# Attention outputs of two sequences times their output weights: seven quarter products in place of eight

## The chip, the core and the metric

The kernel runs on one core of a Trainium2 chip. The metric is device time in microseconds (us) of one execution; it is compared by the median of several runs. Names of engines: PE is the matrix engine (TensorE), DVE is VectorE, ACT is ScalarE, POOL is GpSimd, SP is SyncE, which here only starts transfers. "SPq" or "POOLq" in a row is that engine's sequencer starting a DMA.

## The reference

Eight sequences of 128 tokens with 512 features go through three layers. A per-sequence adapter (one 512x512 matrix chosen by an id) is followed by a base product with eight gated low-rank experts; then comes attention with 32 query heads and 8 key/value heads over a paged cache of 512 positions and the 128 new ones, with its output product; then a bottleneck feed-forward layer with 64 gated experts. Everything is float32. The part that the change touches is the last line of attention:

```python
scores = jnp.einsum('bqhd,bkhd->bhqk', q, k_all) * SCALE
scores = jnp.where(valid[:, None, None, :], scores, -1e+30)
probs = jax.nn.softmax(scores, axis=-1)
o = jnp.einsum('bhqk,bkhd->bqhd', probs, v_all)
o = o.reshape(bsz, seqlen, HQ * D)
return jnp.einsum('bse,de->bsd', o, Wo)
```

With `bsz` 8, `seqlen` 128, `HQ` 32, `D` 128, the last line multiplies, for each sequence, a 128x4096 matrix by a 4096x512 matrix.

## The kernel before

**Units.** Attention is cut into 64 units `u`. A unit is one sequence and one key/value head with its 4 query heads (`REP`). The heads are taken in 4 passes (`NQ`); a pass handles 2 key/value heads (`GH`) of all 8 sequences, so a pass has 16 units, and a step `st = u // 2` is one sequence in one pass. Four units with `u % 4` = 0, 1, 2, 3 are therefore two sequences with two heads each; this group has number `k = u // 4`, 16 of them. In what follows c stands for `u % 4`.

**The order.** No scheduler decides: each engine gets its instructions in the order in which the Python code records them, and works through them in that order. `iteration(u)` records, with a software pipeline over units: the page fetches of the next step's keys (`gather`, L194, on SP; 10 pages in even units and 6 in odd ones, three of them ahead of `exchange_in`), the transfers that bring the previous unit's transposed probabilities back (`exchange_in`, L893 and L896, on SP), the value rows (`gather_v`, L204, on POOL), the rotation tables for an odd unit (`make_tables`, L233, on POOL), in even units the load of the output sums of two steps ahead (`load_y`, L143, on SP), and the eviction of the attention output of unit u-3 (`evict_o`, L927, on ACT).

Then four head slots h = 0 to 3 follow. In each: the score matmuls (`scores`, L834 for the 512 cached keys, L837 for the 128 new ones, into one of two PSUM buffers), masking with the row minimum on DVE (`mask_exp`, L847) and the exponential on ACT (L858), the division by the sum of the head before (`normalize`, L863 on DVE, L864 on POOL), a transpose of 32x32 blocks of the head two before (`blocks`, L869, DVE), four heads' worth of output product of unit u-3 (`output`, L938, one 128x512 matmul a slot), and up to one of the seven products that make queries, keys and values for later units (`project`, L259, 128x384, two matmuls a product; its results are added on DVE in L262). These projections are already computed as seven products of quarters for two sequences at a time; the sums of their inputs' quarters come from `sums_x` (L168 to L171, POOL, once per pair of sequences) and of their weights' quarters from `sums_q` (L163, DVE).

At the end of a unit: the last division and the last two block transposes, `norms(u+3)` (L308 on ACT, L312 and L314 on POOL), `exchange_out(u)` (L883: the transposed probabilities go to DRAM, two transfers from SP, two from ACT), `rotate(u+3)` (L326 to L344 on DVE; the step L340 waits for POOL's L314), one more projection in odd units, and `values(u-2)` (L916, ten 128x512 matmul instructions).

**The output product.** The 8 head products of a step add up in one PSUM bank (`y`). After the second head `add_output` evicts it on DVE: L955 copies in the first pass, L959 adds the sum of earlier passes that `load_y` brought from DRAM, and L962 writes the new sum to DRAM. The sum that `load_y` fetches in unit u is used in unit u+2:

```python
if u % GH == 0 and B <= st - 1 < NQ * B:
    load_y(st - 1)
```

The output weights of a head (`wo_t[g]`, 4x512 columns) sit in one of three buffers and are loaded by `load_o` (L177, POOL queue). In the program a 128x512 float32 matmul is one instruction; the trace shows two matmul records and two weight loads for each, so 256 matmuls of L938 stand there as x512.

Of the kernel before, what the change touches and what calls it, by code (L numbers as in the profile page):

```python
# [57 lines left out]
def adaln_ffn_kernel(  # L58
# [42 lines left out]


# [31 lines left out]
    xo = keep.tile([P, B // 2, 7, 2, S], F32, name="xo")  # L134
    yp = ctx.enter_context(tc.tile_pool(name="yp", bufs=3))
# [5 lines left out]
    def load_y(st):  # L141
        t = yp.tile([P, DM], F32, tag="ya", name=f"ya_{st}")
        nc.sync.dma_start(out=t, in_=y_d[st % B])  # L143
        ya_t[st] = t

    wq_t, wo_t = {}, {}
# [18 lines left out]
    def sums_x(pr):  # L165

        a = xo[:, pr].rearrange("p x c s -> p x (c s)")
        nc.gpsimd.tensor_tensor(a[:, 5], a[:, 0], a[:, 2], ALU.subtract)  # L168
        nc.gpsimd.tensor_tensor(a[:, 2], a[:, 2], a[:, 3], ALU.add)
        nc.gpsimd.tensor_tensor(a[:, 4], a[:, 2], a[:, 0], ALU.subtract)  # L170
        nc.gpsimd.tensor_tensor(a[:, 6], a[:, 1], a[:, 4], ALU.subtract)  # L171

    def load_o(g, first=0, end=REP):

        if first == 0:
            wo_t[g] = wp.tile([P, REP, DM], F32, tag="wo", name=f"wo_{g}", bufs=GH + 1)
        nc.gpsimd.dma_start(  # L177
            out=wo_t[g][:, first:end], in_=wo[g, first:end].rearrange("h p n -> p h n")
        )
# [47 lines left out]
    def make_tables(st):  # L227

        b = st % B
        t = pj.tile([P, 2, 4, D // 2], F32, tag="tab", name=f"tab_{st}", bufs=2)  # L230
        nwv = nw.rearrange("p i (t d) -> p (i t) d", t=2)
        for i, f in enumerate((cos, sin)):
            nc.gpsimd.tensor_tensor(  # L233
                t[:, i], nwv, f[:, b, :].unsqueeze(1).to_broadcast([P, 4, D // 2]), ALU.mult
            )
        tab_t[st] = t
# [12 lines left out]

    def project(k, j, products):  # L250
# [3 lines left out]
        for i in products:  # L254
# [3 lines left out]
            for c in range(2):  # L258
                nc.tensor.matmul(  # L259
                    out=ps, lhsT=xo[:, pr, x, c, :], rhs=w[:, c, :], start=(c == 0), stop=(c == 1)  # L260
# [92 lines left out]
    def transpose_qk(u, home=None):  # L353
# [7 lines left out]
        if home is None:  # L361
            home = pj.tile([P, NH * S], F32, tag="qkT", name=f"qkT_{u}", bufs=2)
# [33 lines left out]
    with ExitStack() as l0:  # L396
# [30 lines left out]
        bias = yp.tile([P, DM], F32, tag="ya", name="bias")  # L427
# [7 lines left out]
        for b in (5, 6, 7):  # L435
            wt_7 = wp.tile([P, NC, DM], F32, tag="wo", name=f"wt_{b}", bufs=GH + 1)
            wt_home[b] = wt_7
# [48 lines left out]
        ang = yp.tile([P, B, D // 2], F32, tag="ya", name="ang")  # L486
        kk = yp.tile([P, B, D // 2], F32, tag="ya", name="kk")
# [126 lines left out]
        for t in range(B):  # L614
# [34 lines left out]
            if t in (5, 6):  # L649
                make_tables(t - 5)  # L650
# [13 lines left out]
        for g in range(GH):  # L664
            load_o(g)
# [3 lines left out]
        rotate(1)  # L669
        l0_experts(B - 1)  # L670
        project_whole(1, 0, 0, 0)
        transpose_qk(1)
# [4 lines left out]
        transpose_qk(2, wt_7.rearrange("p c n -> p (c n)")[:, : NH * S])  # L677
# [110 lines left out]
    with ExitStack() as l1:  # L788
# [8 lines left out]
        p_t, pb_t, pT_t, den_t, o_t, oT_t, y_t = {}, {}, {}, {}, {}, {}, {}  # L797
# [15 lines left out]
        def blocks_qk(u, w):  # L813

            if w == 1:
                gap = xo[:, 0, 4:].rearrange("p x c s -> p (x c s)")[:, : NH * S]
# [82 lines left out]
        def heads_qk(u):  # L899

            qkT = pj.tile([P, NH * S], F32, tag="qkT", name=f"qkT_{u}", bufs=2)
# [22 lines left out]

        def evict_o(u):
            oT = wk1.tile([P, REP, S], F32, tag="oT", name=f"oT_{u}")
            nc.scalar.copy(  # L927
                oT.rearrange("p h (i a) -> p h i a", a=32),
                o_t.pop(u).rearrange("p (i h a) -> p h i a", i=QD, h=REP),
            )  # L930
            oT_t[u] = oT

        def output(u, h):
            st, g = units[u]
            j = g % GH
            if h == 0 and j == 0:
                y_t[st] = bank("y", f"y_{st}")
            nc.tensor.matmul(  # L938
                out=y_t[st],
                lhsT=oT_t[u][:, h, :],  # L940
                rhs=wo_t[g][:, h, :],
# [4 lines left out]
        def add_output(u):  # L946
            st, g = units[u]
            del oT_t[u]
            if g % GH < GH - 1:
                return  # L950
            y = y_t.pop(st)
            last = st >= (NQ - 1) * B
            if g < GH:
                ya_t[st] = yp.tile([P, DM], F32, tag="ya", name=f"ya_{st}")
                nc.vector.tensor_copy(ya_t[st], y)  # L955
            else:

                t = y_home[st % B] if last and st % B < 4 else ya_t[st]
                nc.vector.tensor_tensor(t, y, ya_t[st], ALU.add)  # L959
                ya_t[st] = t  # L960
            if not last:
                nc.sync.dma_start(out=y_d[st % B], in_=ya_t.pop(st))  # L962
# [4 lines left out]
        y_home, yT_t, room_t = {}, {}, {}  # L967
# [44 lines left out]
        spare = xo.rearrange("p r x c s -> p (r x c s)")  # L1012
        written_t = {}

        def z_blocks(b):
            if 0 <= b < TURNED:
                turn_blocks(zg_t[b], spare[:, b * DM : (b + 1) * DM])

        def z_exchange(b):

            if 0 <= b < TURNED:
                written_t[b] = turn_out(b, spare[:, b * DM : (b + 1) * DM])
# [3 lines left out]
        def iteration(u):  # L1026
# [30 lines left out]
            if u % GH == 0 and B <= st - 1 < NQ * B:  # L1057
                load_y(st - 1)
# [10 lines left out]
            for h in range(REP):  # L1069
                if on(u):  # L1070
                    scores(u, h)
                    mask_exp(u, h)
                    if h > 0:
                        normalize(u, h - 1)

                    if h == 1:
                        if u == 2:
# [19 lines left out]
                if on(u - 3):  # L1097
                    output(u - 3, h)
# [5 lines left out]
            if on(u - 3):  # L1104
                add_output(u - 3)
# [5 lines left out]
            if u < NU - 8:  # L1111
                if r in (8, 9, 10, 11):
                    load_q(group + r // 10, r % 2, r % 2 + 2)
                if r in (12, 13):
                    load_o(group, r % 2 * 2, r % 2 * 2 + 2)
# [193 lines left out]
```

## Time and profile before

| | |
|---|---|
| three runs | 1242.72, 1242.82, 1244.57 us; median 1242.82 us |
| profiled execution | 1242.47 us, span in the trace 1240.6 us |
| granted PE clock | 0.999 of full |
| PE busy | 1223.1 us (99% of the span) |
| DVE busy | 905.9 us (73%) |
| POOL busy | 588.7 us (47%) |
| ACT busy | 506.6 us (41%) |
| HBM | 243 GB/s over the span |

The profiled execution is 1.9 us longer than its span, which counts from the first to the last instruction of the program. Busy shares are means over the whole kernel; start (to 115 us), attention (115 to 1200 us) and the end (to 1240.6 us) have different limits. Rows of matmuls overlap their successors by some tenths of a us, so the cost of one is read from start to start. In a group's row the columns are line, engine, operation, output<-input, shapes, count, then busy us and mean ns, then the idle time before it with what ended it.

### The profile page before, as it was taken

Reading aid. Unit: us, or ns where it says so; the run is one execution under the profiler, and the core shown is the slowest. Engines: PE = TensorE matmul, PEld = TensorE weight load, DVE = VectorE, ACT = ScalarE, POOL = GpSimd, SP = SyncE. Lnnn points to the kernel's source line nnn. Section 1 sums busy time; section 2 is a strip of 40 time slices with the busy share of each in tenths; the row PEclk is TensorE's granted clock in tenths of the full one; section 3 lists DMA queues with packets and bytes.
Section 4 is the critical chain, followed back from the end, with each engine's and each line's share of the span. In section 5 each row is a group of like instructions: output and inputs, shape, how many; then the busy total and the mean of one; then the engine's idle time right before and its main releaser. Section 6 shows DMA issues by size and latency. Waiting matters only on the chain.

```text
span 1240.6 us, 15999 instructions
## 1 busy us (share of the span) xinstructions
PE 1223.1 (99%) x3823; PEld 648.6 (52%) x3823; DVE 905.9 (73%) x2051; ACT 506.6 (41%) x1457; POOL 588.7 (47%) x687
## 2 busy tenths in 40 slices
PE   8999899999999999999999999999999999999998
PEld 7765455554555555555555545555555555555544
DVE  2545788888877777788877777799777777787622
ACT  1344544444444444444444444444444444443211
POOL 2443565675544545555545544555545544553100
PEclk9999999999999999999999999999999999999999
DMA  8833687788878877888878877888878776888642
GB/s 303 287 96 94 218 237 247 226 282 281 272 238 256 273 246 239 276 283 278 269 260 257 259 247 248 290 280 288 261 242 280 249 237 220 258 271 268 206 126 95
DMA packets 209825, 302.14 MB, mean 244 GB/s; under 512 B 85123, under 2 KB 120708, under 8 KB 208836
## 3 DMA queue, kind: packets, MB, share of 16 engines
q1 hardware_dynamic: 178132, 208.72, 53.7%
q10 hardware_dynamic: 18720, 52.32, 12.0%
q0 software_dynamic: 12880, 40.08, 9.7%
q8 instruction: 31, 0.51, 0.2%
q14 instruction: 62, 0.51, 0.1%
HBM read 185.12 MB, written 115.93 MB: 243 GB/s over the span
## 4 chain that ended last, share of the span: by engine, by line
PE 92%; DVE 2%; DMA 1%; ACT 1%; SPq 1%; POOL 1%; issue 1%; ACTq 0%; DVEq 0%; POOLq 0%
PE o L916 20%; PE p L259 20%; PE y L938 18%; PE s L834 17%; PE s L837 4%; PE bp L546 2%; PE op L1200 2%; PE p L292 2%; PE cp L524 2%; PE fz L730 2%; DMA bww<-in_base_w 1%; DMA pT<-px 1%; PE cp L541 1%; SPq L883 1%; PE bp L587 0%
## 5 line engine op out<-in xcount | busy, mean ns | idle before, releaser
L864 POOL TENSOR_SCALAR p<-p,den 128x640 f32<-128x640 f32 x256 | 210.9, 824 | 424.3 <-DVE den L863 423.8
L858 ACT ACTIVATE p<-p,low 128x640 f32<-128x640 f32 x256 | 212.0, 828 | 433.0 <-DVE den L863 294.3
L847 DVE CUSTOM_DVE_ANT_0 p<-s,mask,rs 128x640 f32<-128x640 f32 x256 | 223.6, 879 | 109.8 <-PE s L837 106.9
L259 PE MATMUL p<-wqkv,xo 128*128 128x384 f32 x784 | 280.3, 486 | 0.0
L938 PE MATMUL y<-wo,oT 128*128 128x512 f32 x512 | 262.4, 597 | 6.3 <-ACT oT L927 6.3
L834 PE MATMUL s<-kt,qkT 128*128 128x512 f32 x504 | 258.7, 595 | 2.0 <-ACT qkT L903 1.0
L916 PE MATMUL o<-pT,vt 128*128 128x512 f32 x512 | 230.2, 592 | 0.0
L869 DVE STREAM_TRANSPOSE pb<-p 128x640 f32<-128x640 f32 x256 | 210.9, 824 | 17.7 <-POOL p L864 17.7
L259 PEld LDWEIGHTS p<-wqkv,xo 128*128 128x128 f32 x784 | 149.1, 190 | 140.1 <-issue 73.5
L837 PEld LDWEIGHTS s<-qkT 128*128 128x128 f32 x504 | 96.1, 191 | 121.1 <-issue 121.1
L916 PEld LDWEIGHTS o<-pT,vt 128*128 128x128 f32 x512 | 97.3, 190 | 110.3 <-issue 95.2
L204 POOL DMA_INDIRECT vt<-in_vc,vrow x128 | 136.0, 1063 | 39.1 <-issue 28.1
L834 PEld LDWEIGHTS s<-kt,qkT 128*128 128x128 f32 x504 | 95.1, 190 | 96.9 <-issue 53.9
L308 ACT ACTIVATE sq<-c 128x128 f32<-128x128 f32 x320 | 98.8, 309 | 8.1
L314 POOL TENSOR_TENSOR rs<-ss,mhalf 128x5 f32<-128x5 f32 x64 | 99.1, 1548 | 5.3
L837 PE MATMUL s<-qkT 128*128 128x128 f32 x504 | 97.1, 274 | 0.0
L927 ACT COPY oT<-o 128x512 f32<-128x512 f32 x64 | 37.5, 586 | 143.9 <-PE o L916 136.4
L938 PEld LDWEIGHTS y<-wo,oT 128*128 128x128 f32 x512 | 78.6, 192 | 13.2 <-ACT oT L927 8.8
L262 DVE TENSOR_TENSOR c<-c,p 128x384 f32<-128x384 f32 x84 | 45.3, 539 | 30.4 <-PE p L259 30.4
L916 PE MATMUL o<-pT,vn 128*128 128x512 f32 x128 | 65.4, 592 | 0.0
L308 ACT ACTIVATION_READ_ACCUMULATOR sq<-c 128x1 f32 x320 | 59.7, 187 | 0.0
L340 DVE SCALAR_TENSOR_TENSOR ca<-c,rs,tab 128x128 f32<-128x128 f32 x64 | 24.8, 388 | 42.2 <-POOL rs L314 42.2
(183 smaller groups left out, 1199.8 us busy)
## 6 DMA issues: line engine op xcount, KB each, us to landing
pT<-px SPq DMA_DIRECT2D x64, 1280.0 KB, 6.6
px<-pb ACTq DMA_DIRECT2D x120, 400.0 KB, 6.6
px<-pb SPq DMA_DIRECT2D x120, 400.0 KB, 5.4
qkb<-px SPq DMA_DIRECT2D x61, 320.0 KB, 3.5
kt<-in_kc SPq DMA_DIRECT2D x512, 32.0 KB, 4.4
wqkv<-in_wqkv POOLq DMA_DIRECT2D x32, 384.0 KB, 5.0
yd<-ya SPq DMA_DIRECT2D x24, 256.0 KB, 3.0
wo<-in_wo POOLq DMA_DIRECT2D x12, 512.0 KB, 4.5
```

The source lines that it names most:

```text
L204: nc.gpsimd.indirect_dma_start(out=kv_t[step][1][:, c, :], out_offset=None, in_=vc, in_offset=bass.IndirectOffsetOnAxis(ap=vrow[:, hf, at ...
L259: nc.tensor.matmul(out=ps, lhsT=xo[:, pr, x, c, :], rhs=w[:, c, :], start=(c == 0), stop=(c == 1))
L308: nc.scalar.activation(sq, cs[:, at : at + D], AF.Square, accum_out=ss[:, h : h + 1])
L314: nc.gpsimd.tensor_tensor(rs, ss, mhalf, ALU.pow)
L834: nc.tensor.matmul(out=s[:, :L], lhsT=qkT[:, h, :], rhs=kt[:, :, g % GH, :], start=True, stop=True)
L837: nc.tensor.matmul(out=s[:, L:NK], lhsT=qkT[:, h, :], rhs=qkT[:, REP, :], start=True, stop=True)
L847: nc.vector.tensor_tensor_reduce(out=p, in0=s_t.pop((u, h))[:, :NK], in1=mask_t[st], scale=rs_t[u][:, h : h + 1], scalar=BIG, op0=ALU.add, ...
L858: nc.scalar.activation(p, p, AF.Exp, bias=low, scale=-1.0, accum_out=den)
L864: nc.gpsimd.tensor_scalar(p_t[u, h], p_t[u, h], den, 1.0, ALU.mult, ALU.mult)
L869: nc.vector.transpose(pb_t[u][:, :, h * w : (h + 1) * w].rearrange("p i (j a) -> p j i a", a=32), p_t.pop((u, h)).rearrange("p (j i a) -> ...
L916: nc.tensor.matmul(out=o, lhsT=vt[:, c, j * D : (j + 1) * D] if c < LC else vn_t.pop(u), rhs=pT[:, c], start=(c == 0), stop=(c == LC),)
L938: nc.tensor.matmul(out=y_t[st], lhsT=oT_t[u][:, h, :], rhs=wo_t[g][:, h, :], start=(h == 0 and j == 0), stop=(h == REP - 1 and j == GH - 1),)
```

## The change

For 13 of the 16 groups k (all but 0, 14 and 15) the output product of two sequences and two heads is treated as a 2x2 block product, (sequences) x (heads) times (heads) x (halves of the 512 output columns), and is computed with seven products of blocks in place of eight. One product is four 128x256 matmuls (`product_y`), two in each of two head slots; 14 half products lie in 16 head slots. Products alternate between the two halves of one PSUM bank, `y_ps`, which is now one tile for all of attention. Two products are evicted by ACT copies, five by DVE additions, and POOL does two more additions on the results (`combine_y`).

The sums of blocks that the seven products need are made as follows. On the left, `sums_y` makes four sums of 128x512 a group on POOL, in a new tile `ot` with five places, one of which each `evict_o` fills. On the right, the weights of a pass are one tile `wo_t` of seven blocks of 4x256 columns, not buffered twice; `sums_o` makes four sums a pass on DVE, and `load_o` fetches four blocks a pass.

The sums of earlier passes are now added on POOL (`add_y`, 128x512) for groups 4 to 13. The sum of the first sequence of group k is loaded at the start of unit 4k+7, added at the end of unit 4k+8 and stored in 4k+9. The sum of the second is loaded at the start of unit 4k+10, behind that unit's page fetches as before, added in head slot 2 of the same unit, and stored at its end; for group 13 this is unit 61 with c = 1.

To make room, the projection's input sums move from `xo` (7 places per pair of sequences, made once) to `xs` (4 places in all, remade on POOL for each pair and pass in slots 1 and 2 of units with c = 3), the tables and the transposed queries have one buffer in place of two, and other short-lived tiles move.

```diff
+    wo_t = wp.tile([P, 7, REP, DM // 2], F32, name="wo")
...
+    def sums_x(pr, *names):
+
+        a, t = (v.rearrange("p x c s -> p x (c s)") for v in (xo[:, pr], xs))
+        for n in names:
+            to, x, y, op = {
+                3: (t[:, 2], a[:, 0], a[:, 2], ALU.subtract),
+                2: (t[:, 1], a[:, 3], t[:, 2], ALU.subtract),
+                1: (t[:, 0], t[:, 1], a[:, 0], ALU.add),
+                4: (t[:, 3], a[:, 1], t[:, 1], ALU.subtract),
+            }[n]
+            nc.gpsimd.tensor_tensor(to, x, y, op)
...
+    def sums_o(t):
+
+        to, x, y = {3: (5, 3, 1), 2: (4, 5, 0), 4: (6, 2, 4), 1: (1, 1, 0)}[t]
+        nc.vector.tensor_tensor(
+            wo_t[:, to], wo_t[:, x], wo_t[:, y], ALU.add if t == 2 else ALU.subtract
         )
...
-        t = pj.tile([P, 2, 4, D // 2], F32, tag="tab", name=f"tab_{st}", bufs=2)
+        t = pj.tile([P, 2, 4, D // 2], F32, tag="tab", name=f"tab_{st}")
...
+        def sums_y(k, n):
+
+            a = ot.rearrange("p x h s -> p x (h s)")
+            a11, a12 = a[:, k % 2], a[:, 1 - k % 2]
+            to, x, y, op = {
+                3: (a[:, 4], a11, a[:, 2], ALU.subtract),
+                1: (a[:, 2], a[:, 2], a[:, 3], ALU.add),
+                2: (a11, a[:, 2], a11, ALU.subtract),
+                4: (a[:, 4], a12, a11, ALU.subtract),
+            }[n]
+            nc.gpsimd.tensor_tensor(to, x, y, op)
...
+        def product_y(k, i, part):
...
+            ps = y_ps[:, (7 * k + order) % 2 * n :][:, :n]
+            for h in range(2 * part, 2 * part + 2):
+                nc.tensor.matmul(
+                    out=ps, lhsT=ot[:, x, h, :], rhs=wo_t[:, y, h, :], start=(h == 0), stop=(h == 3)
+                )
...
+        def add_y(k, i):
+
+            st = 2 * k + i
+            t = y_home[st % B] if st >= (NQ - 1) * B else ya_t[st]
+            nc.gpsimd.tensor_tensor(t, ya_t[st], n_t.pop((k, i)), ALU.add)
+            ya_t[st] = t
...
+            places = [(1, 4, 3), (1, 5, 1), (2, 6, 0), (2, 6, 1), (7, 6, 2), (7, 6, 3), (6, 7, 1)]
+            places += [(6, 7, 2), (5, 7, 3), (5, 8, 0), (3, 8, 1), (3, 8, 2)]
+            places += [(4, 8, 3)] * 2 if k + 1 in WHOLE_Y else [(4, 9, 2), (4, 9, 3)]
...
+        def pool_y(u, h):
+
+            seven = lambda k: 0 < k < NU // 4 - 2
+            k, c = divmod(u, 4)
+            if c == 1 and h == 1 and seven(k - 1):
+                sums_y(k - 1, 3)
+            if c == 2 and seven(k - 1):
+                if h in (1, 3, 4):
+                    sums_y(k - 1, {1: 1, 3: 2, 4: 4}[h])
+            if c == 3 and h == 3 and seven(k - 1):
+                combine_y(k - 1, 6)
+            if c == 0 and h == 1 and seven(k - 2):
+                combine_y(k - 2, 5)
+            if c == 0 and h == 4 and k - 2 >= NQ and seven(k - 2):
+                add_y(k - 2, 0)
+            last = k - 2 == NU // 4 - 3
+            if c == (1 if last else 2) and h == 2 and k - 2 >= NQ and seven(k - 2):
+                add_y(k - 2, 1)
+
+        def moves_y(u, start):
+
+            k, c = divmod(u, 4)
+            seven = lambda k: 0 < k < NU // 4 - 2
+            if start:
+                if c == 3 and k - 1 >= NQ and seven(k - 1):
+                    load_y(2 * (k - 1))
+                last = k - 2 == NU // 4 - 3
+                if c == (1 if last else 2) and k - 2 >= NQ and seven(k - 2):
+                    load_y(2 * (k - 2) + 1)
...
-            if u % GH == 0 and B <= st - 1 < NQ * B:
-                load_y(st - 1)
+            moves_y(u, True)
...
+                    pool_y(u, h)
+                    if u % 4 == 3 and 1 < (u + 5) // 4 < NU // 4 and h in (1, 2):
+                        sums_x((u + 5) // 4 % (B // 2), *((3, 2), (1, 4))[h - 1])
...
-                if on(u - 3):
-                    output(u - 3, h)
+                for f_out, args in OUT.get((u, h), ()):
+                    f_out(*args)
```

## The prediction

> **What bounds the kernel now.** I read the page first (busy shares, then the chain that ended last), then groups by shape for durations, then timelines of single engines over one unit.
>
> ```profile
> PE 1223.1 (99%) x3823; PEld 648.6 (52%) x3823; DVE 905.9 (73%) x2051; ACT 506.6 (41%) x1457; POOL 588.7 (47%) x687
> ...
> PE o L916 20%; PE p L259 20%; PE y L938 18%; PE s L834 17%; PE s L837 4%; PE bp L546 2%; PE op L1200 2%; PE p L292 2%; PE cp L524 2%; PE fz L730 2%; DMA bww<-in_base_w 1%; DMA pT<-px 1%; PE cp L541 1%; SPq L883 1%; PE bp L587 0%
> ...
> L938 PE MATMUL y<-wo,oT 128*128 128x512 f32 x512 | 262.4, 597 | 6.3 <-ACT oT L927 6.3
> ```
>
> PE is the bound, and 18% of the chain is the work that the change cuts. But a cut counts only while PE is never kept waiting, so the covers matter. PE's timeline in units 30 and 31 (unit 30 begins with its first score matmul at 605.28):
>
> ```profile
> 621.28 1.02 PE L834 MATMUL s<-kt,qkT 128*128 128x512 f32 x2
> 622.14 0.38 PE L837 MATMUL s<-qkT 128*128 128x128 f32 x2
> 622.36 1.02 PE L938 MATMUL y<-wo,oT 128*128 128x512 f32 x2
> 623.22 1.02 PE L834 MATMUL s<-kt,qkT 128*128 128x512 f32 x2
> ...
> 626.45 1.02 PE L834 MATMUL s<-kt,qkT 128*128 128x512 f32 x2
> ```
>
> From start to start two 512-column matmuls take 0.86 us, two of 128 take 0.22. SP's queue in unit 30:
>
> ```profile
> 605.52 4.13 SPq L194 DMA_DIRECT2D kt<-in_kc  x3
> 611.31 0.53 SPq L893 DMA_DIRECT2D qkb<-px  x1
> 611.89 0.63 SPq L896 DMA_DIRECT2D pT<-px  x1
> 613.03 5.40 SPq L194 DMA_DIRECT2D kt<-in_kc  x7
> 618.50 0.40 SPq L143 DMA_DIRECT2D ya<-yd  x1
> ```
>
> The load of the old output sum, recorded at the unit's start, is issued 13.2 us into a unit of 16.0, because ten page fetches and the return of the probabilities stand ahead of it. Before, that costs nothing: its user comes two units later. POOL and DVE in the same unit:
>
> ```profile
> 612.87 0.81 POOL L864 TENSOR_SCALAR p<-p,den 128x640 f32<-128x640 f32 x1 [2.42 <-DVE den L863]
> 616.12 0.81 POOL L864 TENSOR_SCALAR p<-p,den 128x640 f32<-128x640 f32 x1 [2.44 <-DVE den L863]
> 618.51 0.80 POOL L864 TENSOR_SCALAR p<-p,den 128x640 f32<-128x640 f32 x1 [1.58 <-DVE den L863]
> ```
>
> ```profile
> 618.33 0.82 DVE L869 STREAM_TRANSPOSE pb<-p 128x640 f32<-128x640 f32 x1
> 619.34 0.84 DVE L869 STREAM_TRANSPOSE pb<-p 128x640 f32<-128x640 f32 x1 [0.18 <-POOL p L864]
> ...
> 623.32 0.88 DVE L847 CUSTOM_DVE_ANT_0 p<-s,mask,rs 128x640 f32<-128x640 f32 x1
> ```
>
> POOL has gaps of about 2 us a slot, but each division is followed closely by DVE's transpose of the same head, and DVE's queue then leads to the next unit's masks, for which PE's third score matmul of that unit (626.45) waits. The mask at 623.32 ends at 624.3: about 2 us of cover.
>
> **The change part by part.** All times within unit 30's frame are us after its start.
>
> *PE.* A 128x256 matmul record: the rate is linear in columns (430 ns at 512, 110 at 128), so 215; the one row with this shape, L1200, gives 3.6 us for 16, or 225 with its end. A group before: 32 records x 430 ns = 13.76 us. After: 7 products x 4 heads x 2 records x 215 = 12.04. Gain 1.72 us, times 13 groups = 22.4 us. There are 312 more weight loads, of 190 ns each beside 215 ns of matmul; sixteen 128-column matmuls with a load each follow at 122 ns (L524, 1.95 us), so loads do not bind: nothing.
>
> *PSUM halves.* Here a rule speaks against the change. DVE's eviction of 256 columns is about 0.40 us (0.68 at 512, 0.54 at 384), and no row shows PE writing one half of a bank during a read of the other. The Trainium skill, page "PSUM — Partial Sum Buffer", section "PSUM bank collisions raise a hardware error", says that two engines must be kept apart by bank, not by address; and in the instruction order the first matmul of most products does wait for DVE or ACT. So the halves are no double buffer. In slot 3 of units with c = 3 the eviction would end at about 8.6 and PE arrive at 8.6; in slot 3 with c = 0 at 9.3 and 9.5. By the rule 0 to 0.3 us a group, I take 0.1: 1.3 us. Were the halves free of each other it would be 0.
>
> *DVE.* Added: five additions of 0.40 for 13 groups, 26 us, and 16 sums of 1024 columns at about 1.4 (L163: 1.30 mean for 768), 22 us; removed 26 evictions of 0.68, 18 us. Net 30 us on an engine that waits 107 us for score matmuls alone; these are its cover. Nothing. ACT's two 0.35 us copies a group are covered the same way (41% busy).
>
> *POOL.* 128x512 additions cost 1.27 (L575), 128x256 about 0.75 (L168 to L171). Added: 4 x 1.27 and 2 x 0.75 for 13 groups, 20 `add_y` of 1.27, 56 input sums of 0.75 less 16 removed ones; some 143 us in total, to 60% busy. In slots each fits its 2 us gap. The fullest unit is c = 3: value rows 2.4, tables 1.5, divisions 3.2, input sums 3.0, `combine_y` 0.75, norms 2: 13 of PE's 16.3 us, near 15 where weight loads are started too. Covered, if POOL starts it on time.
>
> *Single buffers.* Tables wait for the rotation of the unit before (ends at 623.32, before POOL is through its value rows at 624.4): nothing. Queries: the copy follows, on ACT, an exponential that already depends on the last score matmul: nothing. At the start of attention the tables of step 1 now follow a rotation, and four weight loads of 0.8 stand before them: 0 to 1 us, I take 0.7.
>
> *The old sum of the second sequence.* This term decides. In nine units with c = 2 (26, 30, ... 58) POOL adds this sum in slot 2, but its load still stands behind ten pages on SP. In the trace that load is issued 12.4 to 15.0 us into these units, 13.2 on average, and lands 2.7 to 4.6 us later in the loop's six shown landings; I take 2.8, since the probabilities' write that now competes will come later. So the data is there at 16.0, and POOL, done with the second division at 8.4, stands still. Behind it are the third division, `sums_y` 2, the fourth division and the norms. From 16.0: addition to 17.3, division 18.2, `sums_y` 19.5, division 20.3, norms 22.5 (L312 0.3, L314 1.6). DVE: last transpose done 21.2 (before: 14.9), the norm-dependent part of the rotation (1.5) done 24.0, first mask of the next unit 25.0 (before: 19.0). PE starts the next unit at 16.0; its second scores end at 18.1, since slot 0 holds no output work now; product 6 waits for `sums_y` 2 until 19.5; with 0.86 and 1.29 it reaches the third scores at 21.7 and waits for the mask until 25.0. Undisturbed it would have been there at 20.2: 4.8 us late. Later in the unit POOL is behind (tables at 27.8, first division 28.6), DVE's transpose and eviction follow, and product 5 waits 0.6 more; then PE's own work covers the rest. 5.4 us a unit, nine times: 48.6 us. POOL also starts weight DMAs in that stretch, two in units 26 and 42, one in 34, 50 and 58, 0.8 each: 5.5 us. For group 13 the load stands in unit 61 behind six pages (10.4 in unit 31) while PE has 3.4 us more work there: between 0 and 6, I take 3. SP's own next work, `exchange_out`, waits for DVE anyway.
>
> *The clock.* At 151 to 156 us PE waits 0.97 and 2.74 us, and then:
>
> ```profile
> 156.20:160.00 3.80, 3.80 (x8) 1.90 (x7) 3.74 (x7) 0.74 (x2) 3.17 (x5) 0.55 0.98 235
> ```
>
> The granted clock is 0.55 over 3.8 us: 1.7 us of work lost. The skill's page "TensorE: Matmul & The Clock Gate", section "Part 1: The HAM clock gate (the "warmup" mystery)", has the clock fall only after a whole idle window of about 3.4 us; by that, waits of 1.4 and 3.3 us cost nothing. By the trace a dip comes after less. By the rule 0, by the trace at most 9 x 1.7 = 15.3; I take half, 7.7.
>
> *Sum.* The profiled execution, 1242.5 (the median of the runs shown is 0.3 higher): - 22.4 + 48.6 + 5.5 + 3 + 7.7 + 1.3 + 0.7 = 1286.9 us.
>
> **The rivals.** *The load comes in time or POOL's wait is absorbed* (faster, 10%): then 1242.5 - 22.4 + 2 = 1222. For it: POOL waits 424 us for DVE as it is. Against: SP's queue order is the same in the changed program, and the wait is in front of a division. It decides at a load landing before 9.7 (8.4 plus a slot's slack); the trace has none before 15. *Only the wait for `sums_y` is felt*, because DVE catches up (5%): nine times 1.4, 1242.5 - 22.4 + 13 + 2 = 1235. *POOL becomes the bound* (8%): L314 takes 1.18 to 1.75 us with what DVE does beside it; if all new additions stretch likewise, c = 3 passes 16.3 and each of 13 groups gives 2 us more: 1287 + 26 = 1313. A landing at 4.6 and all clock dips give about the same (16 + 8 more).
>
> **How the numbers follow.** My forecast has 74%; its own spread, with 3.5 to 8 us a stall, is 1256 to 1312. What a measurement of this kernel can tell from no change is about 0.2%, 2.5 us; 3% remain for that band. Faster: 10 and 5%. The range 1252 to 1314 leaves out the two cases below it and a little above.
>
> **What would show it.** Right: POOL's additions of old sums in units with c = 2 preceded by about 7.5 us of idle time ended by the DMA `ya<-yd`; PE idle in the next units before `y_ps` and before L834's successor; units with c = 3 some 5 us longer than 16.3; groups 1 to 3 at about 64.5 us, later ones near 70; granted clock below 0.99. Wrong: groups 4 to 12 also at 64.5, or PE idle for another reason.

## The result and the profile after

| | before | after |
|---|---|---|
| median of runs | 1243.22 us (4 runs, 1242.72 to 1244.57) | 1309.22 us (4 runs, 1304.95 to 1311.55) |
| ratio | | 1.0521, 95% interval 1.048 to 1.0561 |
| profiled execution, its span | 1242.47, 1240.6 us | 1311.55, 1309.8 us |
| granted PE clock | 0.999 | 0.982 |

The changed kernel is 66 us slower. The page of after, busy shares, chain by engine, the two groups that matter and the row of the granted clock:

```profile
PE 1233.2 (94%) x4135; PEld 717.1 (55%) x4135; DVE 951.2 (73%) x2106; ACT 510.0 (39%) x1483; POOL 742.3 (57%) x828
...
PE 62%; DVE 13%; DMA 9%; POOL 6%; issue 5%; ACT 4%; SPq 1%; ACTq 0%; DVEq 0%; POOLq 0%
...
L991 PE MATMUL y_ps<-wo,ot 128*128 128x256 f32 x728 | 195.0, 392 | 15.3 <-DVE n L1007 7.4
L858 PE MATMUL s<-kt,qkT 128*128 128x512 f32 x496 | 265.2, 617 | 42.4 <-DVE low L871 25.6
...
PEclk9999999999999999989999999989999999989999
```

PE's share fell from 99% to 94%, and DVE, DMA and POOL now hold 28% of the chain. The score matmuls alone (L858) had 42.4 us of idle time ahead of them. Three of forty slices of the clock row show an 8.

The stall that the prediction described stands in unit 30 (begins at 615.2) and unit 31, mostly as it was described. SP, POOL and ACT of unit 30:

```profile
622.35 5.38 SPq L212 DMA_DIRECT2D kt<-in_kc  x7
627.78 0.43 SPq L152 DMA_DIRECT2D ya<-yd  x1
```

```profile
622.75 0.80 POOL L888 TENSOR_SCALAR p<-p,den 128x640 f32<-128x640 f32 x1 [1.19 <-DVE den L887]
630.63 1.26 POOL L1019 TENSOR_TENSOR ya<-ya,n 128x512 f32<-128x512 f32 x1 [7.08 <-DMA ya<-yd]
631.87 0.80 POOL L888 TENSOR_SCALAR p<-p,den 128x640 f32<-128x640 f32 x1
632.64 1.27 POOL L974 TENSOR_TENSOR ot<-ot 128x512 f32<-128x512 f32 x1
```

```profile
631.93 0.37 ACT L1002 COPY n<-y_ps 128x256 f32<-128x256 f32 x1 [5.09 <-POOL ya L1019]
632.20 0.73 ACT L927 COPY qkT<-qkb 128x640 f32<-128x640 f32 x1
```

The load starts behind seven page fetches (three more, and the return of the probabilities, stand ahead of these), 12.6 us into the unit, and POOL starts on it 2.85 us later; POOL has stood 7.08 us. The division behind it (631.87) and `sums_y` 2 (632.64) are late with it. ACT shows something the prediction did not have: its copy of product 7 waits for the tile that POOL is still adding, and the copy of the next unit's queries stands behind that copy. PE in unit 31:

```profile
632.98 1.13 PE L858 MATMUL s<-kt,qkT 128*128 128x512 f32 x2 [1.65 <-ACT qkT L927]
640.09 2.07 PE L858 MATMUL s<-kt,qkT 128*128 128x512 f32 x2 [2.53 <-DVE low L871]
```

DVE of the same stretch:

```profile
632.70 0.84 DVE L893 STREAM_TRANSPOSE pb<-p 128x640 f32<-128x640 f32 x1 [5.01 <-POOL p L888]
634.72 0.84 DVE L893 STREAM_TRANSPOSE pb<-p 128x640 f32<-128x640 f32 x1 [1.17 <-POOL p L888]
...
636.69 1.35 DVE L361 SCALAR_TENSOR_TENSOR ca<-c,rs,tab 128x128 f32<-128x128 f32 x1
...
639.15 0.88 DVE L871 CUSTOM_DVE_ANT_0 p<-s,mask,rs 128x640 f32<-128x640 f32 x1
```

PE waits for the queries and, at the third head, for DVE's mask (639.15), which stands behind the transposes of the late divisions and the rotation. The second PE row takes 2.07 us in place of 1.02: PE has just been put at half clock.

To see where the 66 us are I took, for each PE record, the time to the next record's start less what a record of its width takes undisturbed (430 ns for 512 columns, 322 for 384, 216 for 256, 110 for 128). What is lost at half clock, about half of the time that it lasts, is called half clock below; the rest is called waits. The two spans differ by 69.2 us: work -21.5, half clock +22.0 (23.7 against 1.7), waits +68.6 (90.8 against 22.2).

### The profile page after: what moved, and what is told of

Read it like the earlier page. It is cut to its first block, busy times and chain, and to the rows that moved or that the text cites. A ratio compares the mean times of both kernels' runs of the same rounds, so it can differ in the third digit from the quotient of the medians.

```text
span 1309.8 us, 16899 instructions
## 1 busy us (share of the span) xinstructions
PE 1233.2 (94%) x4135; PEld 717.1 (55%) x4135; DVE 951.2 (73%) x2106; ACT 510.0 (39%) x1483; POOL 742.3 (57%) x828
## 3 DMA queue, kind: packets, MB, share of 16 engines
q10 hardware_dynamic: 18720, 52.32, 11.7%
## 4 chain that ended last, share of the span: by engine, by line
PE 62%; DVE 13%; DMA 9%; POOL 6%; issue 5%; ACT 4%; SPq 1%; ACTq 0%; DVEq 0%; POOLq 0%
PE p L280 13%; PE o L940 12%; PE s L858 11%; PE y_ps L991 8%; DMA pT<-px 4%; PE y_ps L1033 3%; PE s L861 3%; DVE p L871 2%; PE bp L567 2%; PE op L1363 2%; DVE pb L893 2%; DVE ca L361 2%; PE cp L545 2%; PE p L313 2%; POOL p L888 2%
## 5 line engine op out<-in xcount | busy, mean ns | idle before, releaser
L858 PE MATMUL s<-kt,qkT 128*128 128x512 f32 x496 | 265.2, 617 | 42.4 <-DVE low L871 25.6
L871 DVE CUSTOM_DVE_ANT_0 p<-s,mask,rs 128x640 f32<-128x640 f32 x256 | 222.4, 879 | 66.5 <-PE s L861 64.5
L991 PE MATMUL y_ps<-wo,ot 128*128 128x256 f32 x728 | 195.0, 392 | 15.3 <-DVE n L1007 7.4
L280 PE MATMUL p<-wqkv,xs 128*128 128x384 f32 x448 | 160.5, 490 | 4.7 <-DVE c L283 3.7
L858 PEld LDWEIGHTS s<-kt,qkT 128*128 128x128 f32 x496 | 91.2, 195 | 120.1 <-DVE low L871 38.6
L991 PEld LDWEIGHTS y_ps<-wo,ot 128*128 128x128 f32 x728 | 127.9, 196 | 30.0 <-DVE n L1007 6.2
L280 PE MATMUL p<-wqkv,xo 128*128 128x384 f32 x336 | 124.9, 495 | 0.0
L280 PEld LDWEIGHTS p<-wqkv,xs 128*128 128x128 f32 x448 | 85.0, 191 | 50.4 <-DVE c L283 6.2
L954 ACT COPY ot<-o 128x512 f32<-128x512 f32 x64 | 37.5, 585 | 162.1 <-PE o L940 113.5
L335 POOL TENSOR_TENSOR rs<-ss,mhalf 128x5 f32<-128x5 f32 x64 | 86.8, 1356 | 5.3
L280 PEld LDWEIGHTS p<-wqkv,xo 128*128 128x128 f32 x336 | 65.4, 196 | 30.9 <-issue 5.0
L361 DVE SCALAR_TENSOR_TENSOR ca<-c,rs,tab 128x128 f32<-128x128 f32 x64 | 46.0, 719 | 44.7 <-POOL rs L335 44.7
L974 POOL TENSOR_TENSOR ot<-ot 128x512 f32<-128x512 f32 x52 | 70.2, 1350 | 0.0
```

Source lines behind the costliest of these rows:

```text
L280: nc.tensor.matmul(out=ps, lhsT=left(pr, x, c), rhs=w[:, c, :], start=(c == 0), stop=(c == 1))
L335: nc.gpsimd.tensor_tensor(rs, ss, mhalf, ALU.pow)
L858: nc.tensor.matmul(out=s[:, :L], lhsT=qkT[:, h, :], rhs=kt[:, :, g % GH, :], start=True, stop=True)
L871: nc.vector.tensor_tensor_reduce(out=p, in0=s_t.pop((u, h))[:, :NK], in1=mask_t[st], scale=rs_t[u][:, h : h + 1], scalar=BIG, op0=ALU.add, ...
L991: nc.tensor.matmul(out=ps, lhsT=ot[:, x, h, :], rhs=wo_t[:, y, h, :], start=(h == 0), stop=(h == 3))
```

## The experiments

Line numbers shift by some lines between the kernels. All ratios are to the kernel before, on the same chip.

**1. The late load alone, in the kernel before.**

```diff
+                    if h == 2 and u in range(26, 59, 4):
+                        for _ in range(2):
+                            nc.gpsimd.tensor_scalar(ya_t[st - 1], ya_t[st - 1], 1.0, 1.0, ALU.mult, ALU.mult)
```

> One part alone in the kernel before: in units 26, 30 ... 58 POOL multiplies the old sum, whose load is started in the same unit behind the page fetches, twice by one in head slot 2 (2 x 0.64 us, as long as an addition of 128x512); nothing else is changed, no quarter products. Theory (the stall is a cost of the late load, not of the products): POOL stands from about 8 to 16 us of the unit in nine units; without sums_y behind it the first masks of the next unit are 1.3 us earlier than I worked out for the changed kernel, so PE loses 3.3 - 1.3 = about 2 us at the third head plus up to 1.4 in slot 0, 18 to 32 us in nine units, and up to nine clock dips of 1.7 us: 1243 + 18 to 47 = 1261 to 1290. Rival (PE's own work covers a late division when the products are not there): 1243 to 1250.

Measured: 1306.23 us, ratio 1.05 (1.0469 to 1.053). More than expected. Unit 34 and the beginning of 35, POOL, ACT and PE:

```profile
700.02 1.32 POOL L1087 TENSOR_SCALAR ya<-ya 128x512 f32<-128x512 f32 x2 [6.83 <-DMA ya<-yd]
```

```profile
704.62 0.92 ACTq L883 DMA_DIRECT2D px<-pb  x2
705.59 0.59 ACT L927 COPY oT<-o 128x512 f32<-128x512 f32 x1 [6.15 <-DVE pb L869]
```

```profile
706.22 2.08 PE L938 MATMUL y<-wo,oT 128*128 128x512 f32 x2 [4.17 <-ACT oT L927]
```

Here the stall reaches PE by another way: DVE's last transposes are late, ACT's two transfers of `exchange_out` wait for them, and the eviction of the attention output stands behind those on ACT, and it is the output product in slot 0 that needs this eviction. Nine units lose 41.7 us in waits at that one place; half clock rises by 25.5 us. A stall of POOL of about 8 us (70.9 us in all nine units) costs 62 us, without any quarter product.

**2. Its control: the same POOL work on a tile that was loaded two units earlier.**

```diff
-                            nc.gpsimd.tensor_scalar(ya_t[st - 1], ya_t[st - 1], 1.0, 1.0, ALU.mult, ALU.mult)
+                            nc.gpsimd.tensor_scalar(ya_t[st - 2], ya_t[st - 2], 1.0, 1.0, ALU.mult, ALU.mult)
```

> The control of the kernel before with the late load: the same two multiplications by one on POOL in the same nine head slots, on the old sum that was loaded two units earlier. Theory (the 62 us come from waiting for the load, not from 1.3 us of POOL work in the slot): 1243 to 1247 us, no clock dip beyond the first, no wait of POOL for a DMA there. Rival (POOL's queue has no room for 1.3 us more in that slot): some 9 x 1.3 to 9 x 3 us more, 1255 to 1270.

Measured: 1245.4 us, ratio 0.9992 (0.9975 to 1.001). The work costs nothing, the wait costs 62 us.

**3. The changed kernel with the load at the head of its unit, ahead of the page fetches.**

```diff
+            load_second(u)
             if pages:
                 gather(st + 1, first, first + 3)
...
-                if c == (1 if last else 2) and k - 2 >= NQ and seven(k - 2):
-                    load_y(2 * (k - 2) + 1)
```

> One edit to the changed kernel: the load of the second sequence's old sum is started at the head of its unit, ahead of the page fetches, so it should land some 5 us into the unit, before POOL is at the addition (8.4 us). Theory (the late load makes the stall, and the stall makes the clock dips): the mask wait of 29.3 us and the qkT wait of 19.0 us over nine late units go, and most of the twelve extra clock dips of 1.7 us with them, so 1309 - 48 - 17 = about 1244 us; groups 6 to 14 return from about 73 us to 66 to 67 us, and the granted clock to above 0.99. Rival A (POOL is the bound, whatever the load does): groups 6 to 14 stay above 70 us and the time above 1290. Rival B (only the mask wait belongs to the load, the qkT wait and the dips do not): 1309 - 29 = 1280.

Measured: 1279.47 us, ratio 1.0295 (1.0266 to 1.0323): 30 us of the expected 65. POOL's waits for `ya<-yd` are gone from the waits view, and the 42.6 us at the first and third scores of units with c = 3 fell to about 2. But in the same units product 5 (slot 3) now loses 22.3 us. DVE and PE in unit 47:

```profile
910.59 0.84 DVE L844 STREAM_TRANSPOSE pb<-ca 128x640 f32<-128x640 f32 x1 [2.50 <-DMA px<-pb]
911.36 0.80 DVE L893 STREAM_TRANSPOSE pb<-p 128x640 f32<-128x640 f32 x1
912.09 0.38 DVE L1007 TENSOR_TENSOR n<-n,y_ps 128x256 f32<-128x256 f32 x1
```

```profile
912.52 1.74 PE L991 MATMUL y_ps<-wo,ot 128*128 128x256 f32 x4 [2.20 <-DVE n L1007]
```

Product 6 is done, but its eviction stands in DVE's queue behind a transpose into the tile that the previous unit's probabilities are still being written from, and product 5, in the other half of the bank, waits for the eviction. In the changed kernel product 5 lost only 1.0 us there, so the stall had covered this wait. Neither of the two rivals named it. With the load in time the change is still 2.95% slower.

**4. ACT's link cut: product 7 is copied by DVE, the load stays late.**

```diff
-                nc.scalar.copy(n_t[k, 1][:, n:], ps)
+                nc.vector.tensor_copy(n_t[k, 1][:, n:], ps)
```

> One edit to the changed kernel: product 7 is copied out of PSUM by DVE instead of ACT. The late load stays. DVE waits for POOL's division at that point anyway, so the copy's wait for the tile that POOL still adds no longer holds up ACT, and the copy of the transposed queries behind it on ACT runs in time. Theory (the ACT link only covers a wait that the late sums_y 2 would make, 1.4 us): the 19.0 us of qkT waits become about 9 x 1.4 = 13 us before product 6, the mask wait stays at 3.3 us a unit, and the time falls by about 6 us, to 1303. Rival (the ACT link is a cost of its own): the time falls by 19 us or more, to 1290 or below.

Measured: 1318.37 us, ratio 1.0607 (1.0578 to 1.0636), slower than the changed kernel. Both expectations failed. (The profiled execution, 1312.78 us, is the fastest of its four and only 1.2 us longer than that of after, so most of the 9 us is in no trace.) The waits view, first after, then this kernel (engine, line and what it waited for; total us, times, longest):

```profile
PE s L858 <- DVE low L871: 26.3, 12, 4.1
PE s L858 <- ACT qkT L927: 16.7, 10, 2.7
```

```profile
PE s L858 <- DVE low L871: 40.1, 12, 5.2
...
PE y_ps L991 <- POOL ot L974: 3.7, 4, 1.4
```

The wait for the queries is gone, the mask wait has grown by nearly as much, and product 6 now waits for `sums_y` 2. The mask of the third head comes when DVE's chain lets it; whatever PE waits before, it waits less there. Waits that all end ahead of the same late event do not add.

**5. A second bank: products 3, 4 and 6 in the bank of the attention output, on top of experiment 3.**

```diff
+            if i in (3, 4, 6):
+                if part == 0:
+                    po_t[k, i] = bank("o", f"po_{k}_{i}")
+                ps = po_t[k, i][:, :n]
+            else:
+                ps = y_ps[:, int(i in (2, 5)) * n :][:, :n]
```

> The kernel with the load ahead of the page fetches, and products 3, 4 and 6 written to the bank that the attention output uses between units, the other four to the two halves of their own bank as before; only products 2 and 7 still follow each other in one bank. Theory (the halves of one bank are no double buffer; the waits for the eviction of the other half cost over 1 us a group): beside the kernel with the load first, 13 groups x 1 to 1.5 us = 13 to 20 us less, 1225 to 1231. Rival (what groups 3 to 5 lack of their 1.72 us is lost on DVE, POOL or at the masks, not at the bank): under 4 us less, about 1241.

Measured: 1256.45 us, ratio 1.0104 (1.008 to 1.0128): 23 us less than experiment 3. What the products lose at evictions fell from 42.7 to 17.5 us, and half clock from 10.1 to 3.4. So in this program halves of one bank were no double buffer. (Experiment 7 narrows this: there product 6 is back in a half beside product 5, and the wait does not return once its eviction is early in DVE's queue. The shared bank and DVE's order make the wait together.) New in the waits view is product 6 waiting for ACT to empty the borrowed bank, and the projections for DVE:

```profile
PE p L280 <- DVE c L283: 7.6, 6, 2.6
PE po L996 <- ACT ot L954: 7.1, 12, 0.7
```

**6. Three moves on top of it.** POOL's addition of the first old sum from the unit's end to slot 3:

```diff
-            if c == 0 and h == 4 and k - 2 >= NQ and seven(k - 2):
+            if c == 0 and h == 3 and k - 2 >= NQ and seven(k - 2):
```

> The kernel with two banks and the early load (1256 us), and one move more: POOL adds the old sum of the first sequence in head slot 3 of units with c = 0 instead of after the norms at the unit's end. Theory (at the end of a unit POOL's 128x512 addition runs beside DVE's rotation, whose first step with two multiplied operands then takes 1.37 us instead of 0.35, so DVE is a full 1 us late with the next unit's masks): in the ten units with c = 1 from unit 25 on that step falls back to 0.35 us and the mask and bank waits of c = 1 (2.2 and 2.8 us in late units) mostly go: 3 to 5 us less, 1251 to 1253. Rival (the step takes long for another reason, such as its table being written late): the step stays at 1.37 and the time within 1 us of 1256.

Product 6 a slot earlier and back in its own bank:

```diff
-            places = [(1, 4, 3), (1, 5, 1), (2, 6, 0), (2, 6, 1), (7, 6, 2), (7, 6, 3), (6, 7, 1)]
-            places += [(6, 7, 2), (5, 7, 3), (5, 8, 0), (3, 8, 1), (3, 8, 2)]
+            places = [(1, 4, 3), (1, 5, 1), (2, 6, 0), (2, 6, 1), (7, 6, 2), (7, 6, 3), (6, 7, 0)]
+            places += [(6, 7, 1), (5, 7, 3), (5, 8, 0), (3, 8, 1), (3, 8, 2)]
```

> The kernel with two banks and the early load (1256 us), with product 6 a head slot earlier (slots 0 and 1 of c = 3) and back in its own bank, half apart from product 7. In the kernel with two banks product 6 waits 0.8 us in slot 1 for ACT's copy of the attention output out of the shared bank, 7.1 us in late units and 3.4 in early ones. Theory: both go, and product 5 doesn't wait for product 6, whose eviction now stands ahead of the transpose that waits for the probabilities' write on DVE: 1256 - 10 = 1246 us. Rival (product 6 in slot 0 meets sums_y 2, which POOL is late with, and waits as long): 1254 to 1258.

Both, and the fourth weight sum a unit earlier:

```diff
-                        if r in (5, 6, 7, 9) if u > 16 else r in (6, 7, 8, 9):
-                            sums_o({5: 3, 6: 2, 7: 1, 9: 4}[r] if u > 16 else (3, 2, 1, 4)[r - 6])
+                        if r in (5, 6, 7, 8) if u > 16 else r in (6, 7, 8, 9):
+                            sums_o({5: 3, 6: 2, 7: 1, 8: 4}[r] if u > 16 else (3, 2, 1, 4)[r - 6])
```

> Both moves together, and the fourth sum of the output weights one unit earlier (unit 16p+8 instead of 16p+9, where product 4 of the first group of a pass waits 1.3 us for it, three times). If the three are independent: 1256 - 4 - 10 - 4 = 1238 us, under the kernel before (1243). Rival (waits of PE stand in for each other as in the kernel with product 7 copied by DVE, because the next mask on DVE sets the unit's end): 1246 or more.

Measured: 1263.35 (ratio 1.0137, 1.009 to 1.0184), 1259.05 (1.009, 1.0061 to 1.0119) and 1261.8 us (1.0114, 1.0063 to 1.0164). None is faster than experiment 5 beyond the intervals, though the first two removed what they aimed at. In the first, DVE's step with two multiplied operands did get shorter; groups of experiment 5, then of this kernel (the last number before the second bar is the mean in ns):

```profile
L361 DVE SCALAR_TENSOR_TENSOR ca<-c,rs,tab 128x128 f32<-128x128 f32 x64 | 46.1, 720 | 59.6 <-POOL rs L335 59.6
```

```profile
L361 DVE SCALAR_TENSOR_TENSOR ca<-c,rs,tab 128x128 f32<-128x128 f32 x64 | 36.0, 562 | 53.8 <-POOL rs L335 53.8
```

That is 10 us over 64 steps, what ten steps of 1.37 in place of 0.35 us come to. But PE's waits in units with c = 1 grew from 18.2 to 22.5 us (product 4 and the projections, L280, lose more). In the second, product 6's 10.5 us went, and the projections in slot 3 of c = 3 went from 5.0 to 10.1 us. (The profiled execution of the second, 1266.76 us, is the slowest of its seven; in that of the third, 1261.42 us, these projections lose 10.7 us.)

**7. DVE's order: in slot 2 the products (and with them their evictions) ahead of the two transposes; product 6 in its own bank in its old slots; the fourth weight sum a unit earlier.**

```diff
+                if h == 2:
+                    for f_out, args in OUT.get((u, h), ()):
+                        f_out(*args)
...
-                for f_out, args in OUT.get((u, h), ()):
-                    f_out(*args)
+                if h != 2:
+                    for f_out, args in OUT.get((u, h), ()):
+                        f_out(*args)
```

> The kernel with two banks and the early load (1256 us), with three edits: product 6 back in its own bank in its old slots 1 and 2 (so it doesn't wait for ACT's copy of the attention output), in head slot 2 the products are recorded ahead of DVE's two block transposes (so product 6's eviction is not queued behind the transpose that waits for the probabilities' write), and the fourth sum of the output weights one unit earlier. POOL's addition of the first old sum stays at the unit's end. Theory (DVE's in-order queue, not the number of banks, makes the wait between products 6 and 5): the 7.1 + 3.4 us in slot 1 of c = 3 go without a wait in slot 3, and 4 us at three pass starts: 1256 - 14 = 1242 us. Rival (every wait removed on PE comes back at the next eviction, since DVE's chain of a unit has no slack left): 1254 or more.

And with the projection of slot 2 ahead of the transposes too:

```diff
+                if h == 2 and slots:
+                    project(k, j, slots[1:2])
...
-                if h > 0 and slots:
+                if h in (1, 3) and slots:
```

> The same with the projection of head slot 2 recorded ahead of the transposes as well, in all units. Theory: the waits of slot 3's projections for DVE's evictions (2 to 5 us in early c = 1 and c = 3 units, as much in late ones) fall, 1242 - 5 = 1237. Rival (DVE now waits for PE's projection with the transposes queued behind it, which the exchange of the probabilities needs): slower than the same without it, 1245 or more.

Measured: 1255.31 us (ratio 1.007, 1.0043 to 1.0097) and 1285.68 us (1.031, 1.0279 to 1.0342). In the first, products lose only 4.8 us at evictions, down from 17.5, yet all waits of PE stay at 56.7 us against 55.9. They are now spread over many small ones; five of them:

```profile
PE p L280 <- DVE c L283: 6.9, 5, 2.6
PE s L858 <- DVE low L871: 5.2, 6, 1.7
...
PE s L858 <- DMA kt<-in_kc: 2.9, 2, 2.5
PE y_ps L996 <- DVE n L1012: 2.9, 6, 1.0
PE s L858 <- DMA px<-pb: 2.4, 1, 2.4
```

The second shows the price of the same trick once too often: DVE's waits for the projections' products (L283 for L280) grew from 11.7 to 49.7 us, the transposes behind them are late, and masks with them.

```profile
PE s L858 <- DVE low L871: 33.0, 27, 1.7
```

**8. On top of the first kernel of 7, SP's order: the first sum stored right after the probabilities' return, the second's old sum loaded at the end of the unit before. With it goes one edit not shown: in the first pass the fourth weight sum moves to unit 7.**

```diff
-            load_second(u)
             if pages:
                 gather(st + 1, first, first + 3)
             if on(u - 1):
                 exchange_in(u - 1)
+            store_first(u)
...
-            elif c in (1, 2) and seven(k - 2):
-                store_y(k - 2, c - 1)
+            elif c == 1 and k - 2 < NU // 4 - 3:
+                load_y(2 * (k - 2) + 1)
+            elif c == 2 and seven(k - 2):
+                store_y(k - 2, 1)
```

> The kernel of products recorded ahead of the transposes (1255 us), with SP's order mended: in units with c = 1 the first sequence's sum is stored right after the probabilities are fetched back, ahead of the remaining pages, and the second sequence's old sum is loaded at that unit's end, so that no load at a unit's head waits for a store to land while page fetches and the return of the probabilities stand behind it (in the kernel before it PE waits 7.3 us for this at the first scores of units with c = 2, 2.6 us of it in unit 34, with one clock dip); and the fourth sum of the output weights of the first pass is made in unit 7 instead of 9. Theory: those 7.3 us, a dip of 1.7 and up to 2.8 us in unit 9 go: 1255 - 11 = about 1244 us, the time of the kernel before. Rival (the 1.7 us wait of the store and the earlier transfers collide with the probabilities' return in c = 1 instead): 1252 or more.

Measured: 1266.12 us, ratio 1.0173 (1.0147 to 1.02), slower than experiment 7. The wait at the first scores of late units with c = 2 is 6.7 us (before this edit 7.3), now mostly in units 26 and 42, about 2.5 and 3 us, where it ends with a transfer of key pages. So the load at the unit's head was not its only cause; why the pages are late in some of these units and not in others is open. The profiled execution, 1260.38 us, is the fastest of six, so what makes the others longer is open too.

No version came below the kernel before. The best, the first of 7, is 0.7% above it; experiment 5 and the versions of 6 are 0.9 to 1.4% above it.

## Why the prediction was right, and where its sizes were off

It said slower, 1287 us (1252 to 1314), by a load that is late for POOL. The sign and the stall with its places were right, and experiments 1 and 2 show that such a wait alone makes as much in the kernel before, though by another path to PE. In the changed kernel taking it away brought 30 us (experiment 3).

Two things were not foreseen. "This term decides" was wrong for the sign: its own sum with the load in time was 1222 us, a gain, and experiment 3, in which the load is in time, measured 1279.47, a loss. And the forecast of +44 was 22 us short. The range held the result partly by luck: its width stood for stalls of 3.5 to 8 us each, they came out at 4.7, below the forecast, and what carried the time towards the upper end were the clock and the bank. By its own steps:

| step | forecast | measured |
|---|---|---|
| PE work | -22.4 | -21.5 |
| stall of the second old sum, nine units | +48.6 (5.4 each) | +42.6 (4.7 each) |
| unit 61, POOL's transfers, the start | +9.2 | about +1 to 2: tail and start of attention lose 1.2 us more than before; the transfers show nowhere by themselves |
| clock | +7.7 | +22.0 |
| halves of the bank | +1.3 | about +16: products and whole outputs lose 23.1 us ahead of a matmul, output products before 6.6 |
| the rest (projections, masks in c = 1) | 0 | about +8 |

*PE work* came out: 216 ns for 256 columns against the 215 worked out, and weight loads did not bind.

*The stall* was right in size and partly wrong in its links. The mask wait at the third head was given as 3.3 us and, half clock taken off, is 2.7 in the mean. The wait of 1.4 us for `sums_y` 2 did not appear, since PE waits 2.0 us for the queries first. ACT's copy of product 7 into a tile of one buffer had been costed at nothing ("covered the same way"), and so had the copy of the queries behind it. What failed there is looking at ACT's busy share and not at what its copies wait for and what stands behind them. Experiment 4 shows that this link carried no cost of its own: without it the mask takes the wait over. On DVE the part of the rotation that needs the norms took 2.5 us (636.69 to 639.15) where 1.5 had been set, 1.0 of it because its first step ran beside POOL's `sums_y` 4 (last section).

*The clock* was the largest miss by a single cause. The step "half of nine times 1.7" should have been the whole of it and more: each of the nine stalls is followed by a dip, three of them two windows long, 12 windows and 20 us in all; one more dip, at 264.6 us, makes up the rest. The windows view of after around the wait at 636 to 640, in stretches of 3.41 us (the columns are length, busy PE, PEld, DVE, ACT, POOL, granted clock, DMA share, GB/s):

```profile
633.29:636.70 3.41, 3.41 (x14) 2.16 (x13) 2.24 (x5) 1.87 (x9) 2.94 (x5) 1.00 0.15 40
636.70:640.12 3.42, 0.89 (x4) 0.22 (x2) 3.39 (x8) 0.64 (x2) 2.94 (x3) 1.00 1.00 335
640.12:643.53 3.41, 3.41 (x7) 2.20 (x8) 1.79 (x7) 2.04 (x5) 3.31 (x6) 0.50 0.76 226
643.53:646.94 3.41, 3.41 (x14) 2.27 (x14) 2.95 (x6) 0.92 (x2) 2.88 (x4) 1.00 0.70 208
```

PE was busy 0.89 us of 3.42, and the next stretch is granted half the clock, for its whole length and no longer. The Trainium skill, page "TensorE: Matmul & The Clock Gate", section "Part 1: The HAM clock gate (the "warmup" mystery)", describes a free-running window of 3413 ns, and the traces agree: in each kernel's trace the dips in attention start on one grid of 3.413 us and last one or two such windows. That a window must be idle as a whole is not what the runs show. I took all windows at full clock in the thirteen traces, from 115 us to 41 us before the end. Of 58 that were followed by a dip, 54 had 1.94 us or more of PE idle time, only 9 of them the whole 3.41; four had 1.33 to 1.84. Of 4,087 that were followed by none, none had over 2.01. So an estimate for this kernel, from these windows: over 2 us of idle time in sum within one window costs 1.7 us more for each window of the dip that follows, whether it is one wait or two.

*The bank.* The rule of the PSUM page, as the prediction weighed it, was the right side of that weighing (PE waits for the other half's eviction because the program orders it so; no run left the order out), but its price was worked out from when the matmuls arrive (0 to 0.3 us a group), with evictions where the order alone would put them. The evictions were later. In c = 3 DVE's queue holds a transpose that waits for a transfer (experiment 3). In c = 1 DVE is 1 us late, since the rotation's step took 1.37 us; POOL and DVE of after at 670 us:

```profile
670.68 1.26 POOL L1019 TENSOR_TENSOR ya<-ya,n 128x512 f32<-128x512 f32 x1
```

```profile
670.73 1.37 DVE L361 SCALAR_TENSOR_TENSOR ca<-c,rs,tab 128x128 f32<-128x128 f32 x1 [1.37 <-POOL rs L335]
```

That step alone did not set PE's waits there: with it back at 0.35 us they rose (experiment 6).

*The check by groups.* Groups 1 to 3 were to be at about 64.5 us. They are at 65.1, 69.6 and 66.2, before 66.3, 67.3 and 66.3; group 2 has the dip at 264.6 us in it. So where there is no stall, two of three groups do not get the 1.72 us either. Group 4 of the first kernel of experiment 7, at 64.65 us, had next to no waits, and shows that the gain exists. Elsewhere most waits that were taken away came back at something else that PE needs (experiments 4, 6, 7). What holds the last 34 us of waits (56.7 against 22.2 before, first kernel of 7) is in part DVE: its waits view puts 16.6 us down to DVE, 9.9 to ACT, 5.8 to a DMA and 2.5 to POOL; before, these were 0.8, 10.0, 1.7 and 1.4. That DVE's order as a whole holds them is argued and not shown; a kernel with DVE relieved was not run.

## What to carry to other kernels

Before moving an addition to another engine, look at the place of its load in the issuing queue: one tile that came about 8 us late for an engine that works in order cost 62 us in nine units, and the work itself nothing. Then work out the time with that wait taken away as well: here the change was still a loss. Cost waits by the last event of the unit, not one by one: here a wait removed ahead of a late mask only lengthened the mask's. And when PE's work shrinks, see where every eviction stands in its engine's queue, since PE arrives there earlier and finds what its own work or an earlier wait used to cover.

## What the hardware showed that was not expected

In these traces the granted clock falls by whole windows on a fixed grid of 3.413 us, nearly always after about 2 us or more of PE idle time in the window before (numbers above); in the changed kernel 47.8 us ran at half clock, in the kernel before 3.4.

A DVE operation with two tensor operands in SBUF was held up while POOL ran an addition of two tensors. In the changed kernel the first step of the rotation (L361) takes 0.35 us, but 1.36 in all 23 units in which a POOL addition of 128x512 runs beside it: ten times `add_y`, thirteen times `sums_y` 4, among them all nine units of the stall. Moving `add_y` brought the ten steps back (experiment 6); the thirteen stayed. The weight sums on DVE show it too (minimum, median and maximum in ns):

```profile
L195 DVE TENSOR_TENSOR wo<-wo x16: 1204/1285/3695, 210.0 to 1112.1; 128x1024 f32<-128x1024 f32 x16
```

The longest, at 459.77 us, stands through three POOL operations that follow each other. It goes the other way as well: a division on POOL of 0.80 us that starts just after such a sum takes 1.68. DVE's additions that read PSUM (L283, 0.54 us) are as long beside POOL as alone. The Trainium skill, page "GPSIMD Engine Reference", section "8. Key points", names the shared SBUF interfaces and contention with DVE instructions that have two SBUF inputs; the prediction had looked at POOL's durations for this and not at DVE's.
